# A second, grouped load of x and 32x32 block turns on VectorE for the covariance sums of a two-layer kernel

## The chip, the cores and the metric

The kernel runs on one core of a Trainium2 chip. The metric is the device time of one execution in microseconds. The core has TensorE (PE in the profile, with its weight loads as PEld), VectorE (DVE), ScalarE (ACT), GpSimd (POOL) and SyncE (SP), which here issues nearly all DMAs.

## The reference, cut to what matters

x is (8, 256, 96, 96) in float32: 8 images of 256 channels and 96 x 96 points. Two layers are computed, each added to its input.

```python
# layer 0, on n = groupnorm(x), 32 groups of 8 channels
q, k, v = (fft2(conv1x1(n, w, b)) for (w, b) in ((w1, b1), (w2, b2), (w3, b3)))
q, k = unit_length(q), unit_length(k)            # over the 9216 points of a channel
attn = einsum('bhcn,bhdn->bhcd', q, k) * temperature      # 8 heads of 32 channels
attn = complex(softmax(real(attn)), softmax(imag(attn)))
out = abs(ifft2(einsum('bhcd,bhdn->bhcn', attn, v)))
x = x + conv1x1(out, w_out)
# layer 1, on n = groupnorm(x): linear attention over points
q, k = softplus(conv1x1(n, Wq, bq)), softplus(conv1x1(n, Wk, bk))     # 32 channels
v = conv1x1(n, Wv, bv)
x = x + (q @ (k @ v)) / (q . sum(k))
```

The kernel never makes a Fourier transform of the points. For layer 0 it needs two things from x: the covariance of the channels, of x with itself and of x with x mirrored in both axes (point (h, w) against (-h, -w)), from which the softmax is worked out; and an image y, each row of x multiplied by a 96 x 96 table of that row.

## The kernel before, in words

**Stages.** Each image b goes through five stages. `pair_sums(b)` makes the covariance from even and odd sums of x and its mirror. `attention(b)` turns it into the small matrix mz, woven with `rotate(b)`, which makes y. `images(b)` multiplies y by mz (z, L747), squares, adds and takes roots (e, L788, L792, L793, L794), projects by wo (po, L759) and adds to x (L761). `layer1(b)` makes keys and queries (kq, L844), their softplus, transposed x (xT, L907), and kx (L885). `output(b)` multiplies out (o, L997), adds to x (L1002 on VectorE; L1005 and L1006 on ScalarE and GpSimd) and stores (L1016). `weave` advances one generator by the numbers that the other yields: `pair_sums(b + 1)` runs between the steps of images, layer1 and output of image b, and `rotate(b)` between the steps of `attention(b)`. x and y of an image lie in two arenas that change roles with each image.

**Sums.** x lies in SBUF with channels on partitions and its rows permuted (`x_col`), so that a block of 8 rows holds four rows and their mirrors. In each of 37 steps an image, GpSimd or ScalarE copies the mirrored part (`back`, L381), TensorE transposes front and back (eoT, L403 and L404), ScalarE evicts both (L405, 128x512), VectorE (L419) and GpSimd (L417) make sum and difference, and eight records of products (acc, L337) add up. `bn_stats` on VectorE (L290) takes the statistics of layer 0's norm, and layer 1's. For b > 0 the evicted rows of part of the image (blocks t of 4 and above) are spilled to DRAM (xtd, L409), and the column w = 0 is collected, transposed and spilled apart. The last sums of an image come after its output stage, in a tail of five steps.

**Rotation.** The order of rows is the hand-written list `pieces`. A row that was spilled comes back from DRAM (xT<-xtd, L648); any other one is transposed by TensorE (xr, L662) and evicted by ScalarE (L675). A y matmul (L665) uses the row and its table tm, which in image 0 comes as a window of rt or rb in DRAM and is written to rx, and later is read from rx (L620). Evictions take y (L671) and an extra column (ys, L670).

**Order.** The DMAs of SyncE are issued in the order of the code on one queue. DVE and POOL have a written order in image 0's sums, PE and POOL in attention and rotation, and all five engines in output and the tail; in images and layer1 a scheduler sets it. At the start come the loads of x (L143), the tables with the small loads and wo (`tables`, `load_small`, L233).

**Layer norm.** `group_norm` waits for bn_aggr (mv, L299), and its matmuls gm and gv (L306, L308) average over groups. layer1 begins with it (gm_b), attention too (gm_a).

Of the kernel before, what the change touches and what calls it, by code (L numbers as in the profile page):

```python
# [57 lines left out]
P = 128  # L58
# [5 lines left out]
T0 = 4  # L64
# [8 lines left out]
def two_layer_kernel(ctx: ExitStack, tc: tile.TileContext, x, w1t, b1, w2t, b2, w3, b3, wot, temp,  # L73
# [11 lines left out]
    assert C == KC * P and H == W and TW == 2 * CH and NT == 2 * NS and NC == 2 * NT and W <= P and H % TR == 0  # L85
# [12 lines left out]
    arenas = [const.tile([P, KC, HW], F32, name=f"arena{i}") for i in range(2)]  # L98
# [7 lines left out]
    def x_col(h):  # L106

        if h < H // 2:
            t, r = divmod(h, PR)
        elif h == H // 2:  # L110
            t, r = 0, 2 * PR - 1
        else:
            t = (H - h) // PR
            r = 2 * PR - 1 - (H - h) % PR
        return ((NT - 1 - t) * ROWS + r) * W

    def chunk_rows(c):

        t, half = NT - 1 - c // 2, c % 2
        if not half:  # L120
            return [(PR * t, PR)]
        return [(H - PR * t - PR + 1, PR)] if t else [(H - PR + 1, PR - 1), (H // 2, 1)]

# [3 lines left out]
    def ring_tile(name):  # L127
        return ring.tile([P, 6 * C], F32, tag="ring", name=name)
# [4 lines left out]
    loaded = set()  # L133

    def load_x(b, t):
        loaded.add((b, t))
        if (b, t) == (0, NT - 1):
            for h in (H // 2 - PR, H // 2 + PR - 1, H // 2 - 2, H // 2 + 1):
                nc.sync.dma_start(out=x_of(b)[:, :, x_col(h):x_col(h) + 2 * W], in_=x_v[b, :, :, h * W:(h + 2) * W])
            return  # L140
        for c in (2 * (NT - 1 - t), 2 * (NT - 1 - t) + 1):
            for h, n in chunk_rows(c):
                nc.sync.dma_start(out=x_of(b)[:, :, x_col(h):x_col(h) + n * W], in_=x_v[b, :, :, h * W:(h + n) * W])  # L143
# [4 lines left out]
    for t in range(NT - 1, -1, -1):  # L148
        load_x(0, t)
# [23 lines left out]
    turn = [0]  # L173

    def sum_slot():

        turn[0] += 1
        return xT[:, NX - 2 + turn[0] % 2]


# [7 lines left out]
    pw = const.tile([P, 4], F32, name="pw")  # L188
    nc.vector.memset(pw[:, 3:4], 0.0)
    for j in range(4):  # L190
        nc.vector.memset(pw[32 * j:32 * j + (16, 16, 17, 1)[j], 3:4], 1.0)
        if j != 2:
            nc.vector.memset(pw[32 * j:32 * j + 1, 3:4], 0.5 ** 0.5)
    nc.vector.scalar_tensor_tensor(pw[:, 3:4], in0=ident[:, 80:81], scalar=0.5 ** 0.5 - 1.0, in1=pw[:, 3:4],
                                   op0=ALU.mult, op1=ALU.add)
    for j in range(3):
        nc.vector.tensor_scalar(pw[:, j:j + 1], ident[:, 95 - 32 * j:96 - 32 * j], scalar1=-1.0, scalar2=1.0,
                                op0=ALU.mult, op1=ALU.add)
    nc.vector.tensor_sub(pw[:, 2:3], pw[:, 2:3], ident[:, P - 1:P])
# [47 lines left out]
    rb = dram.tile([H, 2 * W], F32, name="rb")  # L247
    rx = dram.tile([H // TR, W, TR, W + 1], F32, name="rx")

    xtd = dram.tile([2, (H // 2 - PR * T0 + 1) * W, C], F32, name="xtd")  # L250

    def tables():
# [18 lines left out]
        for i in range(2):  # L271
            o = (3 + i) * W
            nc.vector.tensor_copy(t0[:, o:o + 1], r0[:, 0:1])
            nc.vector.tensor_copy(t0[:, o + 1:o + W], r0[:, W - 1:0:-1])
            nc.sync.dma_start(out=rb[:, i * W:(i + 1) * W], in_=r0)
        nc.sync.dma_start(out=rt, in_=t0[:, 3 * W:5 * W])
        load_small()

    def window(h, n, back):

        v = (rb if back else rt)[h:h + n, 0 if back else 1:]
        return bass.AP(v.tensor, v.offset, [[1, W], [2 * W, n], [1, W]])

    def turned(c, h, w):

        return xtd[c, (h - PR * T0) * W + w:]

# [4 lines left out]
    def new_stats(name):  # L292
        return two.tile([P, KC, NC, 6], F32, tag="st", name=name)
# [29 lines left out]
    def image(t):  # L323
        return t.rearrange("p k (h w) -> p k h w", w=W)

    s0 = {}
    evicted = {}

    def pair_sums(b):

        st0 = new_stats(f"st0_{b}")
        acc = [acc_tile(f"acc{c}_{b}") for c in range(2)]

        def products(t, np_, first, last):
            for c in range(2):
                for m in range(KC):
                    mm = nc.tensor.matmul(acc[c][:, m * C:m * C + (KC - m) * P], lhsT=t[0:np_, c, m * P:(m + 1) * P],  # L337
                                          rhs=t[0:np_, c, m * P:C], start=(first and m == 0), stop=(last and c == 1),
                                          skip_group_check=True)
                    if first and m:  # L340
                        tc.keep_in_program_order(mm)

        x = x_of(b)

        w0 = one.tile([P, KC, H + 1], F32, tag="ys", name=f"w0_{b}")
        nc.gpsimd.memset(w0[:, :, H // 2:H // 2 + 1 + PR * T0], 0.0)

        def sides(t, j):

            o = (NT - 1 - t) * TW + (t == 0) * W + 1 + P * j  # L350
            e = (NT - t) * TW - (t == 0) * W - 1 - P * j
            if t or j < 2:
                return [(0, P, x[:, :, o:o + P], x[:, :, e:e - P:-1])]
            m = H // 2
            rows = [x[:, :, x_col(h):x_col(h) + W] for h in (0, H // 2)] + [w0]
            if j == 2:
                return [(0, 32, x[:, :, o:o + 32], x[:, :, e:e - 32:-1])] + [
                    (32 * i + 32, 32, v[:, :, 1:33], v[:, :, W - 1:W - 33:-1] if i < 2 else w0[:, :, m + 2:m + 34])
                    for i, v in enumerate(rows)]

            return [(32 * i, 32, v[:, :, m:m + 32], v[:, :, m:m - 32:-1]) for i, v in enumerate(rows[0:2])] + [
                (64, 32, w0[:, :, 32:64], None), (64, 16, None, w0[:, :, m + 33:m + 49]), (80, 16, None, w0[:, :, m:m + 16]),
                (96, 32, rows[0][:, :, 0:32], rows[0][:, :, 0:32])]

        back = three.tile([P, TR * (W + 1)], F32, tag="tm", name=f"back_{b}")[:, 0:2 * C].rearrange(
            "p (i k n) -> p i k n", i=2, k=KC)

        def turn_back(i):

            t, j = steps[i]  # L370
            assert (b, t) in loaded
            if j == 0:
                xts.append(ring_tile(f"xt_{b}_{t}_{j}").rearrange("p (j c n) -> p j c n", j=3, c=2))
            ab = sides(t, j)
            ready = len(ab) == 1

            front = ab[0][2] if ready else xts[-1][:, j % 3, 0].rearrange("p (k n) -> p k n", k=KC)
            for p0, n, *v in ab:
                for c in range(ready, 2):
                    if v[c] is not None:  # L380
                        (nc.scalar.copy if b and t < 5 and (ready or not c) else nc.gpsimd.tensor_copy)(  # L381
                            (front, back[:, i % 2])[c][:, :, p0:p0 + n], v[c])
            if j == 0:
                col = x[:, :, (NT - 1 - t) * TW:(NT - t) * TW:W]
                h, o = PR * t, H // 2 + 1 + PR * t
                nc.gpsimd.tensor_copy(w0[:, :, h:h + PR], col[:, :, 0:PR])
                if t:
                    nc.gpsimd.tensor_copy(w0[:, :, o:o + PR], col[:, :, :PR - 1:-1])
                else:
                    nc.gpsimd.tensor_copy(w0[:, :, o:o + 1], col[:, :, 0:1])  # L390
                    nc.gpsimd.tensor_copy(w0[:, :, o + 1:o + PR], col[:, :, 2 * PR - 2:PR - 1:-1])
                    nc.gpsimd.tensor_copy(w0[:, :, o - 1:o], col[:, :, 2 * PR - 1:])
            return front, xts[-1][:, j % 3]

        steps = [(t, j) for t in range(NT - 1, -1, -1) for j in range(3)] + [(0, 3)]
        pending, first = None, True
        xts = []
        ahead = turn_back(0)
        for i, (t, j) in enumerate(steps):
            front, both = ahead  # L400
            pt = ps_tile(f"eoT_{b}_{t}_{j}").rearrange("p (c n) -> p c n", c=2)
            for k in range(KC):
                nc.tensor.transpose(pt[:, 0, k * P:(k + 1) * P], front[:, k], ident)  # L403
                nc.tensor.transpose(pt[:, 1, k * P:(k + 1) * P], back[:, i % 2, k], ident)  # L404
            nc.scalar.activation(both, pt, AF.Copy, scale=pw[:, j:j + 1])  # L405
            evicted[0] = both
            if b and t >= T0:
                for c in range(2):
# [198 lines left out]
    def rotate(b):  # L607
# [88 lines left out]
        for p in pending:  # L696
            step(None, p)
# [404 lines left out]
```

## Time and profile before

| | us |
|---|---|
| median of 3 runs | 2705.23 (2702.59 to 2705.66) |
| profiled execution, span | 2700.8 |
| what lies around the span (median less span) | 4.4 |
| PE busy in it | 2659.0 (98%) |
| DVE, ACT, POOL busy | 1916.3, 1357.6, 889.3 |
| image 0: sums start, end; rotation ends | 10.3, 78.8, 152 |
| image 1: attention and rotation | 421.9 to 484.9 |
| image 1: images; layer 1; output; tail of the sums | to 624; 630 to 702; 711.5 to 744.3; to 753.6 |
| attention starts of images 2 to 7 | 753.6, 1084.2, 1414.9, 1745.6, 2076.9, 2407.8 |
| DMA, mean over the span | 105 GB/s, 33.8% of 16 engines |

From one attention to the next it is 330.7 us. The span is the time from the first to the last instruction of one execution. An engine is busy while one of its instructions runs; matmuls overlap, so that the busy time of a single matmul is longer than the step it takes. Lines such as L337 are those of the kernel before. A line of a group has the instruction's output and inputs by the program's names, its shape and count, then busy time and mean ns, then the idle time of the engine ahead of it, with what released it.

### The profile page before, as it was taken

Reading aid. Unit: us, or ns where it says so; the run is one execution under the profiler, and the core shown is the slowest. Engines: PE = TensorE matmul, PEld = TensorE weight load, DVE = VectorE, ACT = ScalarE, POOL = GpSimd, SP = SyncE. Lnnn points to the kernel's source line nnn. Section 1 sums busy time; section 2 is a strip of 40 time slices with the busy share of each in tenths; the row PEclk is TensorE's granted clock in tenths of the full one; section 3 lists DMA queues with packets and bytes.
Section 4 is the critical chain, followed back from the end, with each engine's and each line's share of the span. In section 5 each row is a group of like instructions: output and inputs, shape, how many; then the busy total and the mean of one; then the engine's idle time right before and its main releaser. Section 6 shows DMA issues by size and latency. Waiting matters only on the chain. (4 is left out here: it accounts for less than half of the span.)

```text
span 2700.8 us, 47703 instructions
## 1 busy us (share of the span) xinstructions
PE 2659.0 (98%) x17494; PEld 1905.6 (71%) x17494; DVE 1916.3 (71%) x4092; ACT 1357.6 (50%) x2167; POOL 889.3 (33%) x1335
## 2 busy tenths in 40 slices
PE   8999999999999999999999999999999999999988
PEld 8965678656796567956778567785677856778546
DVE  5678576785768757687666876769657687576766
ACT  3455553456535565355642556435464355644554
POOL 6133431334313344044340442404424134241311
PEclk9999999999999999999999999999999999999997
DMA  5220166302662026520364203641037411373003
GB/s 177 67 60 18 62 191 208 87 12 69 215 182 67 11 81 232 152 71 17 97 221 135 70 26 102 225 134 54 30 105 236 122 48 38 105 240 86 1 7 141
DMA packets 243183, 283.59 MB, mean 105 GB/s; under 512 B 37380, under 2 KB 231240, under 8 KB 242952
## 3 DMA queue, kind: packets, MB, share of 16 engines
q1 hardware_dynamic: 242008, 280.22, 33.8%
q8 instruction: 140, 2.29, 0.4%
q14 instruction: 91, 0.75, 0.1%
q10 hardware_dynamic: 944, 0.34, 0.0%
HBM read 156.76 MB, written 123.72 MB: 104 GB/s over the span
## 5 line engine op out<-in xcount | busy, mean ns | idle before, releaser
L747 PE MATMUL z<-arena,mz 128*128 128x384 f32 (+2 forms) x2400 | 595.0, 476 | 0.0
L793 POOL TENSOR_TENSOR e<-e 128x768 f32<-128x768 f32 x192 | 348.4, 1815 | 553.7 <-ACT e L792 550.1
L759 PE MATMUL po<-e,wo 128*128 128x384 f32 x1536 | 529.8, 486 | 0.2 <-ACT e L794 0.2
L747 PEld LDWEIGHTS z<-arena,mz 128*128 128x128 f32 (+1 forms) x2400 | 325.6, 163 | 241.4 <-issue 42.4
L337 PE MATMUL acc<-xT 128*128 128x256 f32 (+1 forms) x2368 | 448.3, 330 | 2.8 <-POOL xT L417 1.8
L759 PEld LDWEIGHTS po<-e,wo 128*128 128x128 f32 x1536 | 289.4, 190 | 197.7 <-DVE arena L761 1.2
L788 DVE TENSOR_TENSOR e<-z,xT 128x768 f32<-128x768 f32 x384 | 365.8, 953 | 85.4 <-PE z L747 85.3
L290 DVE BATCH_NORM_STATS2 st<-arena 128x6 f32<-128x384 f32 x768 | 410.4, 553 | 12.6 <-DMA arena<-in_x_dram 2.0
L337 PEld LDWEIGHTS acc<-xT 128*128 128x128 f32 x2368 | 382.7, 191 | 45.2 <-DVE xT L419 6.2
L665 PE MATMUL y<-tm,xT 96*128 96x97 f32 x3040 | 406.4, 270 | 3.6 <-DMA xT<-xtd 1.6
L665 PEld LDWEIGHTS y<-tm,xT 96*128 96x128 f32 x3040 | 395.5, 192 | 20.5 <-issue 12.1
L794 ACT ACTIVATE e<-e 128x768 f32<-128x768 f32 x192 | 162.0, 844 | 336.1 <-POOL e L793 333.9
L792 ACT ACTIVATE e<-e 128x1536 f32<-128x1536 f32 x192 | 284.5, 1482 | 91.8 <-DVE e L788 90.3
L405 ACT ACTIVATE xt<-eoT,pw 128x512 f32<-128x512 f32 x296 | 203.5, 688 | 182.9 <-PE eoT L404 171.1
L417 POOL TENSOR_TENSOR xT<-xt 128x256 f32<-128x256 f32 x352 | 256.5, 745 | 72.7 <-ACT xt L405 71.1
L761 DVE TENSOR_TENSOR arena<-arena,po 128x384 f32<-128x384 f32 x384 | 211.1, 552 | 90.9 <-PE po L759 67.7
L670 DVE COPY ys<-y 128x4 f32<-128x4 f32 (+1 forms) x384 | 61.4, 161 | 160.6 <-PE y L665 159.0
L1006 POOL TENSOR_TENSOR arena<-arena,po 128x384 f32<-128x384 f32 x96 | 96.3, 1003 | 232.4 <-ACT po L1005 229.6
L381 POOL COPY back<-arena 128x256 f32<-128x256 f32 (+1 forms) x230 | 84.7, 374 | 267.2 <-PE eoT L404 255.3
L671 DVE COPY arena<-y 128x384 f32<-128x384 f32 (+1 forms) x314 | 171.4, 546 | 1.4 <-issue 1.4
L419 DVE SCALAR_TENSOR_TENSOR xT<-eoT,pw,xt 128x256 f32<-128x256 f32 x240 | 107.2, 478 | 87.9 <-ACT xt L405 87.8
L1002 DVE TENSOR_TENSOR arena<-arena,o 128x384 f32<-128x384 f32 x288 | 142.4, 549 | 38.3 <-PE o L997 38.2
(235 smaller groups left out, 3316.0 us busy)
## 6 DMA issues: line engine op xcount, KB each, us to landing
out_dram<-arena SPq DMA_DIRECT2D x184, 384.0 KB
arena<-in_x_dram SPq DMA_DIRECT2D x182, 384.0 KB
xtd<-xt SPq DMA_DIRECT2D x336, 128.0 KB
xT<-xtd SPq DMA_DIRECT2D x217, 192.0 KB
tm<-rx SPq DMA_DIRECT2D x106, 218.2 KB
rx<-tm SPq DMA_DIRECT2D x16, 218.2 KB
tm<-rt SPq DMA_DIRECT2D x16, 216.0 KB
arena<-in_x_dram SPq DMA_DIRECT2D x8, 288.0 KB
```

What stands on the lines that cost most here:

```text
L290: nc.vector.bn_stats(out=st[:, k, c, :], in_=x_of(b)[:, k, c * CH:(c + 1) * CH])
L337: mm = nc.tensor.matmul(acc[c][:, m * C:m * C + (KC - m) * P], lhsT=t[0:np_, c, m * P:(m + 1) * P], rhs=t[0:np_, c, m * P:C], start=(first ...
L405: nc.scalar.activation(both, pt, AF.Copy, scale=pw[:, j:j + 1])
L417: on_pool(eo[:, c], both[:, 0], both[:, 1])
L665: nc.tensor.matmul(pu[:, o:o + W + 1], lhsT=gt[0:W, 1 - r if back else r, k * P:(k + 1) * P], rhs=tm[:, g % TR + r, :], start=True, stop=True)
L671: (nc.scalar.copy if on_scalar else nc.vector.tensor_copy)(y[:, :, :, g + r:g + 2], src[:, :, 0:W, r:2] if back else src[:, :, W - 1::-1, ...
L747: mm = nc.tensor.matmul(out[:, o:o + n * W], lhsT=columns(mz, k, c, j), rhs=y[:, k, h * W:(h + n) * W], start=(k == 0 and o == 0), stop=(k ...
L759: nc.tensor.matmul(po[:, 0:CH], lhsT=wo[:, k, m * P:(m + 1) * P], rhs=e[:, k, :], start=(k == 0), stop=(k == KC - 1))
L761: nc.vector.tensor_add(x[:, m, n], x[:, m, n], po[:, 0:CH])
L788: nc.vector.tensor_add(e[:, 2 * c:2 * c + 2, :].rearrange("p t (q h) -> p t q h", h=H), pz[:, 0:CH].rearrange("p (q h) -> p q h", h=H).uns ...
L792: nc.scalar.activation(e, e, AF.Square)
L793: nc.gpsimd.tensor_add(e[:, 0:2, :], e[:, 0:2, :], e[:, 2:4, :])
```

## The change: what it does

x is read from DRAM a second time, for the sums alone, in another layout. A "grouped" load puts 32 channels of one block on 32 partitions, and four rows, 12 apart, on the four groups of 32 partitions (`load_grouped`): for each of six v one gets two rows of each group forward (runs of 768 bytes) and their mirrors (runs of 384 bytes), 12 DMAs, and GpSimd copies the wrap column. VectorE turns 32x32 blocks (`turn_blocks`), two instructions of 128x768 for each u, after which rows of points lie on partitions. Both results are written to DRAM (xtd), and a pair of GpSimd and VectorE instructions make sum and difference, 128x768. There are 12 u of three products steps each, and a last step for the middle row: 37 steps, as before.

Gone are eoT and its evictions, the back copies, the spilling of part of the rows, the x permutation, rb, the windows, bn_stats for layer 0, xr and its evictions. The norm of layer 0 comes from acc, which gets a column of ones for the channels' sums, and the diagonal of the covariance. In the rotation every row comes from xtd and the tables from rx; all tables are written in image 0's `tables`. x itself is loaded in natural order during the rotation (8 blocks) and images (4). y has one more column, which takes the place of ys.

```diff
+    def load_grouped(b, v):
+        f, g = staged(b, v)
+        xs = x[b].rearrange("(c i) h w -> i c h w", i=32)
+        if 2 * v == NG:
...
+            nc.gpsimd.tensor_copy(g[0:32, :, 31:32], f[0:32, :, 0:1])
+            return
+        for a in range(G):
+            h, s = NG * a + 2 * v, slice(32 * a, 32 * a + 32)
+            nc.sync.dma_start(out=f[s].rearrange("p c r w -> p c (r w)"), in_=xs[:, :, h:h + 2].rearrange("p c r w -> p c (r w)"))
+            for r in range(2):
+                nc.sync.dma_start(out=g[s, :, r, 0:W], in_=xs[:, :, (H - h - r) % H])
+        nc.gpsimd.tensor_copy(g[:, :, :, W], g[:, :, :, 0])
...
     def tables():
...
-            nc.sync.dma_start(out=rb[:, i * W:(i + 1) * W], in_=r0)
         nc.sync.dma_start(out=rt, in_=t0[:, 3 * W:5 * W])
+        for i in range(NP + 1):
+            n = TR if i < NP else 1
+            tm = tm_tile(f"tm0_{i}")
+            v = rt[TR * i:TR * i + n, 1:]
+            nc.sync.dma_start(out=tm[:, 0:n, 1:W + 1], in_=bass.AP(v.tensor, v.offset, [[1, W], [2 * W, n], [1, W]]))
+            nc.gpsimd.tensor_copy(tm[:, 0:n, 0:1], csn[0:W, 2, TR * i:TR * i + n].unsqueeze(2))
+            nc.gpsimd.tensor_scalar_mul(tm[:, 0:n, W + 1:W + 2], tm[:, 0:n, 0:1], -1.0)
+            if i < NP:
+                for q in range(NQ):
+                    nc.sync.dma_start(out=rx[i].rearrange("(j q) r w -> q j r w", q=NQ)[q], in_=tm[32 * q:32 * q + 32])
...
         load_small()
...
+        def turn_blocks(u):
+            v, r = divmod(u, 2)
+            f, g = staged(b, v)
+            ft, gt = turned_pair(b, u)
+            if u < NG:
+                for t, src in ((ft, f[:, :, r, :]), (gt, g[:, :, r, W:0:-1])):
+                    nc.vector.transpose(out=t.rearrange("p (q c i) -> p q c i", q=NQ, c=NB8),
+                                        in_=src.rearrange("p c (q w) -> p q c w", q=NQ))
+                for c, t in enumerate((ft, gt)):
+                    nc.sync.dma_start(out=xtd[c, u], in_=t)
...
+            if r and v + 2 <= NG // 2:
+                load_grouped(b, v + 2)
+        def pair(u):
...
+            nc.gpsimd.memset(eo[0:np_, 0:nq, :, 0:CB:CB - 1], 1.0 if u < NG else R2)
...
+                nc.gpsimd.tensor_add(e, ft, gt)
+                (nc.gpsimd if b and u % 2 else nc.vector).tensor_sub(o, ft, gt)
+            return eo, nq, np_
+        turn_blocks(0)
+        ahead = pair(0)
+        turn_blocks(1)
+        for u in range(NG + 1):
+            eo, nq, np_ = ahead
+            for q in range(nq):
+                if q == 0 and u < NG:
+                    ahead = pair(u + 1)
+                if q == 1 and u + 2 <= NG:
+                    turn_blocks(u + 2)
...
+                products(eo, q, np_, u == 0 and q == 0, u == NG)
+                yield
...
     def rotate(b):
...
+        tms[0] = load_r(0)
+        tms[1] = load_r(1)
+        for i in range(3):
+            fetch(i)
+        yield
+        for i in range(len(order)):
+            step(i)
             fetch(i + 3)
+            if i % 6 == 3 and i // 6 < NT - 4:
+                load_x(b, i // 6)
             yield
...
     def images(b):
...
+            if i % 2 == 0 and i // 2 < 4:
+                load_x(b, NT - 4 + i // 2)
+            if b + 1 < B and i in (14, 17):
+                load_grouped(b + 1, (i - 14) // 3)
...
             weave(output(b, *l1.pop(b)), sums)
+            finish(sums)
             if b + 1 < B:
                 turns = rotate(b + 1)
-                finish(sums)
+                next(turns)
```

## The prediction

> **What bounds the kernel now.** I read the page's busy line first, then the slices, the costliest groups, the waits, windows by stage, and the timeline of TensorE.
>
> ```profile
> PE 2659.0 (98%) x17494; PEld 1905.6 (71%) x17494; DVE 1916.3 (71%) x4092; ACT 1357.6 (50%) x2167; POOL 889.3 (33%) x1335
> ...
> DMA  5220166302662026520364203641037411373003
> ```
>
> TensorE is busy 98% of 2700.8 us, and its largest wait in the table of waits is 6.2 us in all. So it alone sets the end; work taken from it is time gained, and any idle it gets is time lost. DMA is quiet in most slices but reaches 5 to 7 tenths where images change.
>
> The removed TensorE work, by tile:
>
> ```profile
> L662 PE MATMUL xr<-ident,arena 128*96 128x128 f32 x652 | 167.4, 275 | 0.0
> L403 PE MATMUL eoT<-ident,arena 128*128 128x128 f32 x560 | 147.7, 291 | 5.2 <-DMA arena<-in_x_dram 5.0
> L404 PE MATMUL eoT<-ident,back 128*128 128x128 f32 x592 | 146.6, 274 | 1.6 <-POOL back L381 1.6
> ```
>
> Matmuls are pipelined, so 275 ns is no step; distances between starts count, from the timeline:
>
> ```profile
> 18.74 0.27 PE L403 MATMUL eoT<-ident,arena 128*128 128x128 f32 x1
> ...
> 19.18 1.47 PE L337 MATMUL acc<-xT 128*128 128x256 f32 x8
> 20.49 0.27 PE L403 MATMUL eoT<-ident,arena 128*128 128x128 f32 x1
> ```
>
> A step of the sums takes 1.75 us: four transposes 0.44 (18.74 to 19.18) and the products 1.31.
>
> Windows of image 1 and of the change to image 2 (columns: length, then busy us of PE, PEld, DVE, ACT, POOL, clock, DMA share, GB/s):
>
> ```profile
> 422.00:484.00 62.00, 60.52 (x507) 56.63 (x505) 37.69 (x134) 19.14 (x40) 2.09 (x12) 1.00 0.61 168
> ...
> 706.00:744.00 38.00, 37.86 (x262) 26.50 (x260) 31.57 (x69) 17.37 (x37) 22.34 (x39) 1.00 0.81 277
> 744.00:754.00 10.00, 9.83 (x66) 8.55 (x63) 6.83 (x14) 5.00 (x15) 6.79 (x20) 1.00 0.87 291
> ```
>
> In turn: attention with the rotation; the output stage; its tail of sums. The DMA engines are 81 to 87% busy in the last two; dividing rate by share, the queue would saturate at 275 GB/s with the rotation's mix (168/0.61), 342 with the output's, 334 with the tail's. The reader should see that the change adds transfers where the queue is fullest.
>
> [...] L788, 128x768, takes 953 ns. [...]
>
> **The change, part by part.**
>
> *Gain on TensorE.* Sums: 37 steps x 0.44 = 16.1 us an image. Rotation: image 0 transposes all rows (190 records, 79 to 152, 73 us), image 1 has 66 in 62 us: 11/124 = 0.09 us each. So images 1 to 7 gain 66 x 0.09 = 5.9, image 0 17. That is 22.0 x 7 = 154, and 33 in image 0. The products' extra column (257 wide for 256) is under 0.4%: nothing.
>
> *VectorE, ScalarE, GpSimd in all.* The sums' norm leaves VectorE (half of L290's 410 us), as do L419's 107 and L670's 61. Added are some 200 turns (8 x 25) at 0.95 = 190 us (bounds 0.55, the 384-element copy L671 at 546 ns, and 1.8, if the strided read costs double), some 50 differences of 0.95 to 1.8, and more evictions. VectorE stays near its 71%, ScalarE loses L405's 203 us. On totals nothing new bounds; what matters is what stands ahead of what.
>
> *Image 0.* A pass is two groups u, six steps, 6 x 1.31 = 7.9 us of TensorE. But staged buffers alternate, so the loads for v+2 are issued only after the odd group's turn, and in GpSimd's written order the copy of the wrap column (line 158 of the changed kernel), which waits for these loads, stands before the next pair's sum, and before the memset that VectorE's difference waits for. The loop is: last turn 1.9; 12 issues at 0.39 (the 32 loads of wo took 12.34 us) 4.7; landing 2.1 (the fetch issued at 756.14 was used at 758.2); copy 0.4; sum 1.8 (L793: 1815 ns for 128x768); memset and difference 1.0; turn 1.9: 13.8 us. Over five passes 5 x 5.9 = 29. The tables' nine pieces stand in the same queue: a window, its copy on GpSimd, three writes, about 3.6 us each, 32 us, then wo's 12.3; sums can run some 12 us ahead: 32 more. From a first product at about 14: 14 + 37 x 1.31 + 29 + 32 = 124 where now 78.8: +45. With the rotation's -17: **+28** (bounds 0 and +60).
>
> *Head of layer 1, seven images.* VectorE's order now has pair 0, turns 2 to 4 and differences ahead of the bn_aggr whose result the gm_b matmul (L306) waits for: 6 x 0.95 + 3 x 0.95 = 8.6 us; GpSimd did both sums there. About 1.4 of chain after it, less three steps of products, 3.9: **+6** (1 to 10). [...]
>
> *Output stage.* GpSimd's copy for the middle row (line 151 of the changed kernel) waits for six fresh loads, 6 x 0.39 + 2.1 = 4.4 us plus queueing behind 1.57 MB of output rows; each fourth addition (L1006) and the odd pairs stand behind it: **+3** (1 to 6).
>
> *Start of the rotation.* Behind the last output rows (1.57 MB) in SP's queue come wl (0.79 MB), two tables (0.45) and the first rows (0.4), 3.2 MB: 11 us at 291 GB/s. The tail's cover shrinks from 9.3 us (744.3 to 753.6) to 5 x 1.31 = 6.6. Before, the first rows were turned by TensorE from SBUF, so nothing was needed. 11 - 6.6 = 4.4, landing 2.1, some 1 for a cold clock: **+7.5** (3 to 12).
>
> *Through the rotation.* All 49 steps now fetch: 49 x 192 KB, eight load_x of 768, nine tables of 223: 17.6 MB in binary, 18.0 decimal. At 291 GB/s 62 us, at 275 65, at 342 53. TensorE's need is 62 - 5.9 = 56. Slots prefetch only three to six steps: **+6.5** (0 to 10).
>
> *Covered.* The sums' norm from acc: some eight small VectorE instructions ahead of gm_a, about 2.7 us; woven y steps cover it, else +2.7 an image. The wrap copies of the first two groups, in the images stage, stand between additions L793 whose engine idles 553.7 us before them: nothing, else 2 to 4 us each. load_x into the arena in the rotation has no reader until images: nothing but its bytes, counted above.
>
> Sum for an image: -22.0 + 6 + 3 + 7.5 + 6.5 = +1.0, times 7 = +7, and +28: 2700.8 + 35 = 2736. The median of the runs lies 4.4 above the span: 2740.
>
> **The rivals.**
>
> *The stalls are covered (faster).* One mechanism decides: the queue keeps up. If it moves the rotation's 18.0 MB at 342 GB/s or more, that part takes 53 us under TensorE's 56, the fetches are early, and the start costs 4; with 3 at the head and 2 in the output about 9 an image remain: (9 - 22) x 7 = -91, image 0 +20: 2705.2 - 71 = 2634. It turns at 28/7 = 4 us an image below the gain: with stalls under 18 us an image the kernel is faster. For: output and tail imply over 330; the table shows few waits of y for xT (1.6 us). Against: the rotation's mix implies 275, and those 1.6 us had 22 fetched steps, not 49.
>
> *The queue saturates (much slower).* At 275 or less, [...] rotation +10, start +12, output +6, head +8: 36 an image, (36 - 22) x 7 = +98, image 0 +40: 2843. For: 81 to 87% before anything is added. Against: the grouped loads are spread over some 100 us.
>
> **How the numbers follow.** Forecast (small net loss, 2712 to 2795) 0.46; saturated (2795 to 2870) 0.21; covered (2590 to 2699) 0.28; between, within 0.2% of before, about what a measurement of this kernel can tell from no change, 0.05. Faster 0.28, same 0.05, slower 0.67. The range leaves a tenth out at each end: 2620 to 2840. The cases of slower alone: 2712 to 2840.
>
> **What would show it.** Right: no eoT and xr records; sums at 1.31 us a step; sums of image 0 ending near 124; PE waits at gm_b for mv_b, and at the first y for xT from xtd, of 5 us or more an image; DMA share in the rotation near 1; PE's busy share near 91% (2659 - 187 of 2736). Wrong: image 0's sums ending before 100, a period from sums to sums well under 320 us (now 330.7), or turns far from 0.95 us: at 1.8 VectorE would hold up the head and the sums too.

## The result, and the profile after

| | us | ratio to before, 95% interval |
|---|---|---|
| before | 2705.3 | |
| after | 2973.6 | 1.098 [1.094, 1.101] |

The change makes the kernel 268 us slower. Slower was forecast, but at 2740 and at most 2840. The profiled execution has a span of 2977.4 us. These are its lines of engines, granted clock and DMA on the page:

```profile
PE 2713.5 (91%) x15580; PEld 1931.7 (65%) x15580; DVE 1793.2 (60%) x3294; ACT 1118.8 (38%) x1658; POOL 777.5 (26%) x783
...
PEclk8779997799977999779996899979998799977998
DMA  8673247633386344852457424774157723476003
```

TensorE has 1914 fewer matmul records and is busy for 54.5 us more. Busy time that grows while the work shrinks means slower instructions, and the row PEclk, the share of its full clock that TensorE was granted, says why: before it stood at 9 in all slices but the last (a mean of 0.994), now it dips to 6 or 7 in each image (a mean of 0.896). A stretch at half clock is called cold below. The same shows in the groups (busy us, mean ns, idle before), here with the new transposes:

```profile
L614 PE MATMUL y<-tm,xT 96*128 96x97 f32 x3072 | 523.3, 345 | 116.2 <-DMA xT<-xtd 116.2
...
L339 PE MATMUL acc<-eo 128*128 128x257 f32 (+2 forms) x2368 | 467.1, 346 | 81.4 <-POOL eo L373 68.6
...
L353 DVE STREAM_TRANSPOSE arena<-arena 128x768 f32<-128x768 f32 x192 | 180.7, 959 | 32.9 <-POOL eo L383 22.9
```

The y matmul, unchanged in shape, takes 345 ns in place of 270. From the starts of the stages in both traces (images 2 to 6, mean us):

| | before | after | change | forecast |
|---|---|---|---|---|
| attention and rotation, to the first z | 62.8 | 86.6 | +23.8 | +0.6 |
| images to the end of layer 1 | 225.2 | 222.4 | -2.8 | -3.2 |
| output and tail of the sums | 42.8 | 50.2 | +7.4 | +3.5 |
| period | 330.8 | 359.2 | +28.4 | +1.0 |

(The forecast's 0.44 us a step are shared out by the steps of the sums in each stage before: 21 in the second row, 16 in the third.)

In image 0 attention, which follows the sums, starts at 148.4 us (79.5 before, +69 where +45 was forecast; this start stands for the end of the sums below), and the rotation takes 75.4 us (71.9 before; 17 less was forecast). So most of the loss lies in the rotations. The windows of image 1: rotation, images, output, tail and start of the next rotation (columns as in the prediction's windows; the DMA share can come out above 1):

```profile
499.00:586.00 87.00, 79.38 (x443) 73.82 (x442) 26.79 (x71) 20.40 (x37) 0.20 (x2) 0.70 0.74 219
590.00:731.00 141.00, 139.88 (x530) 81.47 (x528) 113.08 (x172) 72.22 (x79) 56.24 (x40) 0.99 0.26 61
...
811.00:843.00 32.00, 31.65 (x191) 20.95 (x190) 25.35 (x47) 5.26 (x11) 20.79 (x24) 1.00 0.79 279
843.00:861.00 18.00, 7.91 (x47) 7.14 (x43) 5.23 (x15) 0.96 (x2) 1.88 (x6) 0.73 1.03 316
```

In the rotation TensorE idles 7.6 of 87 us and DMA is 74% busy: neither is full. What is low is the clock, 0.70. The timeline of TensorE there:

```profile
496.99 2.85 PE L614 MATMUL y<-tm,xT 96*128 96x97 f32 x12 [10.30 <-DMA xT<-xtd]
...
502.52 7.12 PE L614 MATMUL y<-tm,xT 96*128 96x97 f32 x32
...
516.77 1.96 PE L469 MATMUL cw<-wl,scr 128*128 128x512 f32 x2
...
520.19 1.95 PE L469 MATMUL cw<-wl,scr 128*128 128x512 f32 x4
521.97 1.03 PE L614 MATMUL y<-tm,xT 96*128 96x97 f32 x8
```

After a wait of 10.3 us, 32 y records take 7.12 us (0.22 each, back to back: nothing is waited for). After the wide cw matmuls of attention, 8 take 1.03 (0.11 to the next instruction). The trace's clock records have the granted clock at one half from 489.5 for 30.7 us (it falls within the wait of 10.3), from 544.2 for 20.5 (at the end of a wait of 3.5) and from 574.9 for 17.1 (within the second of two waits, of 1.9 and 2.3). In the first stretch y records, with a few small matmuls of attention between them, run for 20 us and don't end it; it ends 3.5 us after the first cw, the second with mz (264 wide), the third with zs and z.

My first theory was then that of the **clock**: waits for rows, each short, halve TensorE's clock, and the narrow y stream can't win it back. The rival is the **queue**: late rows pace the rotation, and the clock only follows.

### The profile page after: what moved, and what is told of

It is laid out like the page before. It is cut to its first block, busy times and chain, and to the rows that moved or that the text cites. A ratio compares the mean times of both kernels' runs of the same rounds, so it can differ in the third digit from the quotient of the medians.

```text
span 2977.4 us, 41809 instructions
## 1 busy us (share of the span) xinstructions
PE 2713.5 (91%) x15580; PEld 1931.7 (65%) x15580; DVE 1793.2 (60%) x3294; ACT 1118.8 (38%) x1658; POOL 777.5 (26%) x783
## 4 chain that ended last, share of the span: by engine, by line
PE 78%; DMA 8%; DVE 6%; SPq 2%; issue 2%; POOL 2%; ACT 1%; POOLq 0%; ACTq 0%; DVEq 0%
PE z L676 19%; PE po L684 15%; PE y L614 14%; PE acc L339 10%; DMA xT<-xtd 5%; PE kq L771 4%; PE o L916 4%; PE xT L832 3%; PE kx L810 2%; DMA arena<-in_x_dram 1%; DVE arena L803 1%; POOL eo L382 1%; PE cw L469 1%; DVE arena L353 1%; POOL eo L383 1%
## 5 line engine op out<-in xcount | busy, mean ns | idle before, releaser
L614 PE MATMUL y<-tm,xT 96*128 96x97 f32 x3072 | 523.3, 345 | 116.2 <-DMA xT<-xtd 116.2
L676 PE MATMUL z<-arena,mz 128*128 128x384 f32 (+1 forms) x2304 | 602.5, 506 | 0.0
L339 PE MATMUL acc<-eo 128*128 128x257 f32 (+2 forms) x2368 | 467.1, 346 | 81.4 <-POOL eo L373 68.6
L339 PEld LDWEIGHTS acc<-eo 128*128 128x128 f32 (+1 forms) x2368 | 389.8, 198 | 207.4 <-issue 89.0
L619 ACT COPY arena<-y 128x388 f32<-128x388 f32 (+1 forms) x192 | 122.3, 637 | 547.2 <-PE y L614 469.9
L295 DVE BATCH_NORM_STATS2 st<-arena 128x6 f32<-128x384 f32 x384 | 210.6, 554 | 10.3
L353 DVE STREAM_TRANSPOSE arena<-arena 128x768 f32<-128x768 f32 x192 | 180.7, 959 | 32.9 <-POOL eo L383 22.9
L382 POOL TENSOR_TENSOR eo<-arena 128x768 f32<-128x768 f32 x88 | 174.8, 1986 | 7.0 <-DVE arena L353 1.0
L832 PE MATMUL xT<-ident,arena 128*128 128x128 f32 x1152 | 148.7, 278 | 6.0 <-DVE xT L837 3.4
L832 PEld LDWEIGHTS xT<-ident,arena 128*128 128x128 f32 x1152 | 128.7, 143 | 23.2 <-issue 10.7
```

Of the source, the lines that this page charges most:

```text
L295: nc.vector.bn_stats(out=st[:, k, c, :], in_=x_of(b)[:, k, c * CH:(c + 1) * CH])
L339: mm = nc.tensor.matmul(acc[c][:, m * (C + 1):m * (C + 1) + C + 1 - m * P], lhsT=eo[0:np_, q, c, 1 + m * P:1 + (m + 1) * P], rhs=eo[0:np_, ...
L353: nc.vector.transpose(out=t.rearrange("p (q c i) -> p q c i", q=NQ, c=NB8), in_=src.rearrange("p c (q w) -> p q c w", q=NQ))
L614: nc.tensor.matmul(pu[:, o:o + W + 1], lhsT=xt[:, s, k * P:(k + 1) * P], rhs=tm[:, h % TR + s, c:c + W + 1], start=True, stop=True)
L619: (nc.scalar.copy if i % 2 else nc.vector.tensor_copy)(y[:, :, :, g:g + nr], src if c else src[:, :, W::-1, :])
L676: nc.tensor.matmul(out[:, 0:CH], lhsT=columns(mz, k, c, j), rhs=y[:, k, i * CH:(i + 1) * CH], start=(k == 0), stop=(k == KC - 1), skip_gro ...
```

## The experiments

All times are medians on the chip. Each kernel is the changed one with the edit shown, but for the one on the kernel before.

**Fillers ahead of the rotation.**

```diff
+                fill = ps_tile(f"fill_{b}")
+                for _ in range(22):
+                    nc.tensor.matmul(fill, lhsT=ident, rhs=wo.rearrange("p k o -> p (k o)"), start=True, stop=True)
                 turns = rotate(b + 1)
```

> Edit: between the tail of the sums and the first y step of images 1 to 7, where TensorE idles some 10 us, 22 matmuls of 128x512 are added whose result nobody reads (22 x 0.44 us = 9.7 us). Rows arrive no earlier. Clock theory (the idle halves TensorE's clock and the narrow y matmuls, 97 columns wide, don't win it back for 20 us and more): the cold stretch of 30.7 us at the start of each rotation goes; about 22 us of work in it ran at half speed, so about 10 us an image, 70 in all: 2890 to 2920 us, granted clock in the first 20 us of the rotation 1.0. Queue theory (the rotation is paced by rows that come late, and the clock only follows): 2960 to 2980, no shorter rotation than the 82 us of the changed kernel.

Measured 2910.8 us, 1.075 [1.072, 1.077]: 63 less, with 154 matmuls more. The rotation falls from 82 to 67 us; the tail grows by 7, since one such matmul takes 0.88 us and not 0.44 (a matmul shows as two records, of which I had counted one; in the run with five fillers below, five show as 10 records over 4.46 us). The first cold stretch is gone in the clock records. The fillers also hold the first y back by 8 us, in which rows can come; but if rows set the pace, a later start could at best leave the end where it was, and it comes 9 us an image earlier. Clock theory, within its numbers.

**Wide fillers in the rotation, and narrow ones.**

```diff
             pu = ps_tile(f"y_{b}_{c}_{h}")
+            if i % 2 == 0:
+                nc.tensor.matmul(pu, lhsT=ident, rhs=wo.rearrange("p k o -> p (k o)"), start=True, stop=True)
```

> Edit: each second y step gets one 128x512 matmul ahead of its own four, overwritten by them: 25 x 0.44 = 11 us more of TensorE work in each rotation. Clock theory: [...] of some 53 cold us in a rotation 30 to 35 go, saving 16 and costing 11: 2900 to 2960 us, although more work is done; granted clock in the rotation over 0.85 (now 0.70). Queue theory: the work is hidden in waits at best and added at worst: 2980 to 3060, clock below 0.8.

```diff
             pu = ps_tile(f"y_{b}_{c}_{h}")
+            for _ in range(4 if i % 2 == 0 else 0):
+                nc.tensor.matmul(pu[:, 0:W + 1], lhsT=xt[:, 0, 0:P], rhs=tm[:, h % TR, c:c + W + 1], start=True, stop=True)
```

> Edit: as with the wide fillers, but each second y step gets four more matmuls of its own narrow kind (97 columns) in place of one of 512: about the same 0.44 us of TensorE at full clock. Clock theory, that width counts: the clock isn't won back, each filler costs 0.44 to 0.88 us, 25 x 8 of them: 3060 to 3150 us, clock in the rotation 0.7 or below. Theory that any TensorE work wins the clock back: as the wide fillers, 2900 to 2960. Queue theory: 2980 to 3060.

The wide ones: 2941.5 us, 1.087 [1.086, 1.089], 32 us *less* although each rotation has 22 us more work. The narrow ones: 3023.5 us, 1.118 [1.116, 1.119], 50 us more. Their windows in image 1's rotation, wide and then narrow:

```profile
501.00:583.00 82.00, 82.00 (x487) 65.78 (x487) 27.01 (x71) 20.45 (x37) 0.20 (x2) 0.90 0.73 222
```

```profile
510.00:601.00 91.00, 91.00 (x636) 85.51 (x635) 26.75 (x72) 20.60 (x37) 0.21 (x2) 0.82 0.63 194
```

TensorE is busy throughout in both. In image 1's clock records the first cold stretch lasts 23.9 us with wide fillers and 41.0 with narrow ones (30.7 with none). Where it ends says more than its length. With wide fillers it is over before attention's first cw in all seven rotations of images 1 to 7. With narrow ones cw comes later than without fillers (in image 1, 24 us after attention's start in place of 17), and the stretch lasts until 3 to 8 us behind it in all seven. So narrow work doesn't win the clock back, as the clock theory says; whether by its 97 columns or by its 96 rows (128 in the wide matmuls) wasn't separated. It is the clock records that decide here: the time of the narrow ones lies in the queue theory's range and below the clock theory's. Both kinds also remove the later stretches, probably since slower steps let rows come in time, and my numbers for the narrow ones were too high for that reason.

**x loaded behind the rotation.**

```diff
-            if i % 6 == 3 and i // 6 < NT - 4:
-                load_x(b, i // 6)
...
-            if i % 2 == 0 and i // 2 < 4:
-                load_x(b, NT - 4 + i // 2)
+            for t in ((0, 1, 2) if i == 0 else (i // 2 + 2,) if i % 2 == 0 and i // 2 + 2 < NT else ()):
+                load_x(b, t)
```

> Edit: the loads of x in natural order leave the rotation; all but two or three of the twelve blocks are issued behind the last row of the rotation. 4.7 of the rotation's 18 MB go. Queue theory: rows come in time after the start, the rotation falls from 82 to about 65 us: 2840 to 2870. Clock theory: the start is as before (30 us cold), the two later cold stretches shrink or go as their stalls go: 70 to 74 us, 2890 to 2930. If the bytes in the rotation didn't matter: 2970 to 2980.

Measured 2808.0 us, 1.038 [1.036, 1.039]: 166 less, more than either theory had. The rotation takes 64 us, the start is as cold as before (30.7 us in six of the seven images), and no other cold stretch is left in it. So the eight 768 KB loads between the fetches made the later waits (7.6 us in image 1), and these cost far more in clock than they lasted. Both theories have a part: the queue makes the wait, the clock multiplies it. Whether the size of a single load or their bytes in all made the waits was not separated.

**The start on another queue.** wl, two tables and the first six rows, three of them asked for earlier, from ScalarE's queue (nc.scalar.dma_start for b > 0):

> Edit: for images 1 to 7 the three weight loads, two tables and the first six rows of the rotation are issued by ScalarE's DMA queue instead of behind the last output rows in SyncE's. [...] Queue-order theory (the start waits because it stands behind 1.6 MB of output rows in one queue): TensorE's idle at the start falls from 10.3 to 5 us or less; alone -5 x 7 = 2935 to 2950[...]. Bandwidth theory (the bytes need their 10 us whoever issues them): 2965 to 2985.

Measured 2939.5 us, 1.087 [1.084, 1.090]. Output and tail fall from 50 to 45 us, but the rotation stays at 79 to 85 us, with a first cold stretch of 27 to 31: the idle is shorter (5 to 6 us in place of 10 to 12), and the clock drops all the same. Queue order held a part of the start, and not its clock.

**Image 0.** GpSimd's wrap copy just ahead of its turn, and (apart) the tables and small loads on ScalarE:

```diff
-        nc.gpsimd.tensor_copy(g[:, :, :, W], g[:, :, :, 0])
...
             ft, gt = turned_pair(b, u)
+            if r == 0 and u < NG:
+                nc.gpsimd.tensor_copy(g[:, :, :, W], g[:, :, :, 0])
```

> Edit: GpSimd's copy of the wrap column is written just ahead of the turn that reads it, in place of right behind the loads, so that it no longer stands ahead of the next pairs' sums. All images. Theory of the GpSimd order (image 0: passes of 18 us against 8 of products): three to four passes lose 6 to 8 us each: image 0's sums end 20 to 30 us earlier, 2940 to 2955 us. If loads are the limit (12 issues and their landing after the odd turn): under 5 us, 2965 to 2975. Other images within 2 us.

> Edit: the tables' chain (rt, nine windows, 25 writes, two small copies each) and the small loads with wo are issued and done by ScalarE, idle in image 0's sums, in place of SyncE and GpSimd. Theory of the queue (from 64 to 106 us SyncE issues nothing for the sums, and TensorE waits 26.7 and 22.0 us): image 0's sums end 35 to 50 us earlier: 2920 to 2940. If the passes' own loop bounds: 10 to 20 us, 2955 to 2965.

Measured 2940.9 us, 1.087 [1.085, 1.090], and 2931.5 us, 1.083 [1.081, 1.085]. Image 0's sums end at 135 and at 142 us (148 in the changed kernel): 13 and 7 earlier, less than I had for either. That both totals lie in the ranges of the theories which had promised more of the sums is luck. The rest of the first one's gain is 3 us in each later image, where I had expected no change; the rest of the second one's lies in the rotations, image 0's above all (75 to 66 us).

**All four together.**

> Edit: four edits together: x loaded behind the rotation, the start of the rotation on ScalarE's queue, wrap copies late, tables and small loads on ScalarE. Clock and queue theories together: from 2808 (x behind the rotation) image 0 takes 60 to 80 off, the start 5 x 7 = 35, and 10 x 7 more if the start no longer cools the clock: 2640 to 2715, about the kernel before or better. If the edits only shift one wait to another: 2740 or more.

Measured 2780.8 us, 1.027 [1.025, 1.029]: the effects don't add. Image 0's sums end at 124.5, but each rotation of a later image still starts with 27 us of cold clock, though the idle is down to 3.1 us and 1.6 us shortly after (image 2).

**With five fillers, and four more in the first steps.** The four edits together once more, but with the wrap copies late in image 0 alone and the small loads back on SyncE:

> Edit: x behind the rotation, the rotation's start on ScalarE's queue, wrap copies late in image 0 alone, the tables' chain on ScalarE (small loads and wo stay on SyncE), and five wide matmuls without a reader between the sums' tail and the first y step of images 1 to 7 (five take about 4 us, what is left of the idle there). If the clock is the greatest loss: from 2781 with the same edits without fillers, 27 cold us at each start go, 10 x 7 = 70, and 2 x 7 in the output: 2690 to 2715. If fillers only move the wait: 2770 to 2790.

> Edit: as the last combined version (x behind the rotation, start on ScalarE's queue, wrap copies, tables on ScalarE, five fillers before the rotation), and one 128x512 matmul without a reader ahead of each of the first four y steps of images 1 to 7 (4 x 0.88 us at full clock). In that version the clock still drops for 20.5 us a few us into each rotation, after waits of 0.9, 1.1 and 1.1 us among narrow matmuls. Clock theory: with wide work among these waits the clock holds; 10 us saved, 3.5 spent, less what hides in the waits: 6 to 9 us an image, 2710 to 2730. If rows set the pace: 2770 to 2795.

Measured 2769.9 us, 1.023 [1.022, 1.025], and 2780.3 us, 1.030 [1.026, 1.034]. The clock theory's numbers failed in both; the second time lies where rows setting the pace had been expected. The clock still drops for 20.5 us a few us into the rotation. With the start on ScalarE's queue, ScalarE stands at these DMAs (8.4 us for six rows in the trace of all four together) and reaches its part of the norm late: with four more fillers the gv_a matmul waits 2.6 us for ScalarE's dv_a. They cost their time and the clock drops all the same, for 17 to 21 us.

**The same idle in the kernel before.**

```diff
                 finish(sums)
+                stall = ring_tile(f"stall_{b}")[:, 0:3 * C]
+                nc.gpsimd.memset(stall, 0.0)
+                for _ in range(6):
+                    nc.gpsimd.tensor_add(stall, stall, stall)
+                ps = ps_tile(f"stalled_{b}")
+                nc.tensor.matmul(ps[:, 0:P], lhsT=ident, rhs=stall[:, 0:P], start=True, stop=True)
```

> Edit, on the kernel before: ahead of the first rotation step of images 1 to 7, one 128x128 matmul that needs the last of six dependent GpSimd additions of 128x768, whose result nobody reads: TensorE idles some 6 to 8 us there, as in the changed kernel, all else being as before. If one idle of that length costs what it lasts [...]: 7 to 9 us an image, 2755 to 2770. If the rotation can't win the clock back here either: 15 to 18 us an image, 2810 to 2835, with a cold stretch of 20 us and more at each rotation's start.

Measured 2804.4 us, 1.037 [1.035, 1.040]. The timeline shows the idle, and the window after it (image 2) the clock:

```profile
773.13 0.80 PE L1057 MATMUL stalled<-stall,ident 128*128 128x128 f32 x2 [8.72 <-POOL stall L1055]
```

```profile
775.00:838.00 63.00, 62.19 (x513) 58.35 (x512) 37.53 (x133) 19.42 (x40) 0.20 (x2) 0.98 0.52 144
```

An idle of 8.7 us costs 14 us an image: 10 ahead of attention, some 4 through the rotation. The cold stretch lasts 10.2 us in this image and 10 to 17 over the seven, and ends 4 to 11 us after work is taken up again, in each before the first cw. In the changed kernel it is 30.7 in each of the seven and ends 21 to 23 us after. One difference between the two streams is the xr transposes, 128 wide, which are woven into the first steps before and which the change removed. That they bring the clock back is argued from this comparison; no run put them into the changed kernel. Neither of my two numbers fits: the time lies between them, nearer the second.

**x behind the rotation, and fillers to cover the whole idle.** As with x loaded behind the rotation, eleven fillers (11 x 0.88 us) ahead of it, wrap copies late in image 0, tables on ScalarE; the start stays with SyncE.

> Edit: x behind the rotation, wrap copies late in image 0 alone, the tables' chain on ScalarE, and eleven wide matmuls without a reader (11 x 0.88 = 9.7 us) in the idle of 10.3 us ahead of the rotation of images 1 to 7; the start stays on SyncE's queue, so that ScalarE is free for the norm's chain. Clock theory: the bytes that stalled the rotation are gone and the clock enters it full, so no cold stretch is left in it: rotation 54 to 57 us, 8 to 10 us an image less than with x behind the rotation alone (2808), and 18 less in image 0: 2715 to 2735. If the clock drops all the same at the first small wait: 2770 to 2790.

Measured 2740.1 us, 1.014 [1.011, 1.017], the best of the changed design, just above the 2735 expected at most. In four of seven images no cold stretch is left; in three one of 17 to 21 us comes back. Windows of two rotations, and a line of the timeline:

```profile
458.00:515.00 57.00, 56.70 (x485) 52.95 (x489) 26.78 (x72) 20.29 (x37) 0.20 (x2) 1.00 0.85 233
785.00:842.00 57.00, 56.11 (x473) 52.48 (x476) 26.66 (x72) 20.13 (x37) 0.20 (x2) 1.00 0.86 236
```

```profile
808.10 11.83 PE L620 MATMUL y<-tm,xT 96*128 96x97 f32 x104
```

At full clock a y record takes 0.114 us, the rotation 54 to 56 us, and the period is 327 to 328 us in four images (330.8 before). What makes this kernel slower than the one before is image 0: its sums end at 132 us, 52 later, and the rest of the profiled execution is 20 us shorter.

**Why image 0 stays late.** On top of the last version, four staging buffers in place of two in image 0, with four groups loaded at the start; then also the small loads and wo behind the tables on ScalarE:

```diff
-        r = x_of(b)[:, v % 2, 0:LO]
+        r = x_of(b)[:, v % 2, 0:LO] if b or v % 4 < 2 else y_of(b)[:, v % 2, 1024:1024 + LO]
...
-            if r and v + 2 <= NG // 2:
-                load_grouped(b, v + 2)
+            D = 2 if b else 4
+            if r and v + D <= NG // 2:
+                load_grouped(b, v + D)
```

> Edit: the last version (x behind the rotation, wrap copies late in image 0, tables on ScalarE, eleven fillers), and in image 0 four staging buffers in place of two (the two more in the other arena, free there), so that loads run four groups ahead. Theory that the two buffers set image 0's pass (load only after the turn): sums end 20 to 35 us earlier, at 97 to 112 (132 in the last version): 2705 to 2722. Theory that issues and bytes set it (72 loads at 0.45 us, 9.4 MB): under 10 us: 2730 to 2742.

> Edit: as with four staging buffers, and the small loads with wo are issued by ScalarE behind its tables, written three steps into the sums. If the small loads' 47 issues in SyncE's queue (some 19 us) stand ahead of writes that the turns wait for: 10 to 18 us less than with four buffers alone, 2688 to 2710, faster than the kernel before or the same. If the queue has room for them: within 4 us of it.

Measured 2758.5 us, 1.019 [1.017, 1.021], and 2776.2 us, 1.025 [1.022, 1.028]; the sums end at 136 us in both. Two buffers are not the limit. Windows of the first:

```profile
0.00:20.00 20.00, 4.37 (x15) 3.77 (x16) 8.96 (x31) 1.98 (x4) 4.25 (x67) 1.00 0.97 174
20.00:40.00 20.00, 6.46 (x39) 5.77 (x37) 0.67 (x2) 0.00 (x0) 2.06 (x3) 0.76 1.20 211
40.00:60.00 20.00, 14.10 (x73) 12.54 (x74) 13.68 (x33) 0.00 (x0) 10.39 (x11) 0.81 1.00 234
60.00:80.00 20.00, 4.18 (x24) 3.47 (x23) 1.97 (x7) 1.53 (x9) 0.00 (x0) 0.70 0.65 182
80.00:100.00 20.00, 9.86 (x48) 8.66 (x48) 5.00 (x6) 1.22 (x7) 5.41 (x5) 0.76 0.46 126
100.00:120.00 20.00, 5.01 (x17) 4.38 (x18) 8.47 (x10) 0.00 (x0) 6.37 (x6) 0.52 0.55 204
```

The DMA engines are full for 60 us, at 174 to 234 GB/s, and 46 to 65% busy in the next 60. The sums load 9.4 MB in groups and write 9.4 MB to xtd; at these rates 81 to 108 us, an estimate, whatever the order. But bytes don't explain the waits after 60 us. With eleven fillers and two buffers they are plain to see: a window of image 0, SyncE's issues and VectorE's next turn.

```profile
80.00:100.00 20.00, 0.00 (x0) 0.00 (x0) 0.00 (x0) 0.00 (x0) 0.26 (x2) 0.54 0.11 24
```

```profile
87.73 10.80 SPq L233 DMA_DIRECT2D wo<-in_wot_dram  x32
98.63 2.32 SPq L360 DMA_DIRECT2D xtd<-arena  x4
```

```profile
101.16 2.01 DVE L357 STREAM_TRANSPOSE arena<-arena 128x768 f32<-128x768 f32 x2 [32.58 <-DMA xtd<-arena]
```

For 20 us next to nothing runs and DMA is 11% busy: SyncE issues the small loads and wo, 53 DMAs from 77.5 to 98.5 us, and only then the writes to xtd that the turn waits for. With these loads moved to ScalarE, in the last run, SyncE's grouped loads wait 22.4 us for the tables' transfers of the other queue:

```profile
SPq L158 <- DMA tm<-rt: 22.4, 5, 4.8
```

So the order of the issues costs image 0 time that bytes don't explain: with all four edits together, where the small loads are ScalarE's, the sums end at 124.5 us, and with them back on SyncE at 130.8. What else holds image 0 is open. Why the last run is slower still, in its later rotations too (59 to 64 us), I did not settle.

## Why the prediction was wrong

**Right, in part by luck.** A turn takes 959 ns (0.95 forecast, from L788's 953). TensorE's gain is there where the clock is full: with x behind the rotation and eleven fillers it takes 54 to 56 us (forecast: 5.9 less than 60 to 62), image 0's 55.6 in place of 71.9 (-16, forecast -17). Images to the end of layer 1 came out at -2.8 (forecast -3.2), but the wait in it is half of the forecast 6: PE waits 22.9 us in eight images for mv_b at gm_b, 2.9 each, where 5 or more had been named as the sign:

```profile
PE gm_b L311 <- DVE mv_b L304: 22.9, 8, 2.9
```

The rest of what the row lost lies elsewhere: a step more of the sums before output (1.3), a wait at po (1.0), up to 6.8 us at half clock around gm_b. PE's share of 91%, another sign, came out as forecast by chance: 2713.5 us of 2977.4, not 2472 of 2736. The idle at the rotation's start was forecast as 6.5 us before the clock; it is 10.3. Two slips in the working change nothing: 37 x 0.44 is 16.3, not 16.1, and the fetch issued at 756.14 had landed at 758.2, but no y matmul used it then.

**The step that failed** is "some 1 for a cold clock", together with "through the rotation: +6.5". I took the clock for a small surcharge on a wait. From attention's start to the first z the change costs 23.8 us an image where +0.6 was forecast, most of the 28.4 in all. In image 1 the rotation takes 31 us more than at full clock (86 against 55): 7.6 are idle, the other 24 are mostly work at half speed, in stretches of 31, 21 and 17 us that waits of 10, 3.5 and 4 us began. The clock records of both kernels hold two speeds, 1.0 and 0.5. In the changed kernel the stretches at half last 3.4, 6.8, 13.7, 17.1, 20.5, 27.3 or 30.7 us, all multiples of 3.4, but for the last one, which the end of the execution cuts off. Of the way back they show this: y records, with attention's small matmuls between them, run from 497.0 to 516.8 us in image 1 at a granted clock of 0.50; the clock is back 1.8 to 3.5 us after the first cw (128x512) in each of images 1 to 7. What it is in the work that decides was not shown. I had read that TensorE was at full clock in nearly the whole profile of before (three stretches at half clock, of 3.4, 3.4 and 29.2 us, all behind 2609 us), and so saw no price for leaving it. Nor did I ask whether the removed transposes were part of what brings it back, as the idle put into the kernel before suggests.

**Image 0** (+28 forecast, +78 measured: 69 in the sums, where 45 were forecast; 3.5 in the rotation, where 17 were to be gained; the rest behind it). The chain of GpSimd is there; its waits, in the changed kernel's timeline, are these:

```profile
16.81 6.68 PE L339 MATMUL acc<-eo 128*128 128x257 f32 x24 [12.26 <-DVE eo L379]
36.45 11.04 PE L339 MATMUL acc<-eo 128*128 128x257 f32 x48 [12.96 <-POOL eo L373]
54.47 10.57 PE L339 MATMUL acc<-eo 128*128 128x257 f32 x48 [6.98 <-POOL eo L373]
91.72 10.72 PE L339 MATMUL acc<-eo 128*128 128x257 f32 x48 [26.68 <-POOL eo L373]
124.39 22.91 PE L339 MATMUL acc<-eo 128*128 128x257 f32 x128 [21.95 <-POOL eo L373]
```

A pass takes 18 us (33.5 to 51.5 on GpSimd) where I had 13.8, and two waits lie around the tables (68.9 to 121.4). The lines add up to the end of the products, 147.3 where I had 124: the first product comes 3 us later, the four waits after it last 68.6 us in place of 61, and the 37 steps take 61.9 in place of 48.5. So the waits were nearly right, and the largest miss is again the clock, which stands at half for some 20 us of the products. Late copies and other queues together give back 15 to 24 of the 69 us; the cause of what is left stays open. I had priced the grouped loads by their issues, never by the rate at which they move, which fills the DMA engines in the first 20 us (a share of 0.98 at 174 GB/s).

**The rivals.** "The queue saturates" named the place and the sign of what the rotation lost, but as transfer time, 10 us an image; DMA was 74% busy. "The stalls are covered" is the way that x behind the rotation and fillers go: a period 3 to 4 us under the one before in four images, where this rival had 13.

## What to carry to other kernels

What a wait on TensorE cost depended here on the stream behind it: an idle of 8.7 us put into the kernel before cost 14 us an image, with 10 to 17 us at half clock; in the changed kernel one of 10 to 12 us began 30.7 us at half clock in each of seven images. Look at the row of the granted clock, and at what runs after each new wait: y records of 97 columns ran for 20 us at half clock, and after the first cw, of 512 columns, the full clock was back within 1.8 to 3.5 us. Work that is taken from TensorE may also be work that brings its clock back (argued here for the xr transposes, not shown); before removing it, ask what is left behind a wait. Eight loads of 768 KB put between fetches of 192 KB on one queue made waits of 1.9 to 3.5 us here (image 1), and without them the kernel was 166 us faster; put such transfers where no fetch is due. And in a queue that is issued in order, look for small DMAs that nobody needs yet ahead of writes that somebody waits for: 53 of them took SyncE 21 us here, and the turn behind them waited 32.6 us.

## What the runs showed of the hardware

- Wide matmuls without a reader in an idle of TensorE made the kernel 63 us faster (2973.6 to 2910.8), and put between the useful ones of the rotation 32 us faster (2941.5).
- Narrow y matmuls can keep a full clock that they don't win back: with x behind the rotation and fillers, 104 of them ran for 11.83 us at full clock (1.00 in that window); in the changed kernel they ran for 20 us at half (0.50).
- Loads onto 32 partitions at a time, in runs of 768 and 384 bytes, filled the DMA engines (0.97 with four staging buffers, 0.98 in the changed kernel, in the first 20 us) at 174 GB/s; the output stage moved 279 GB/s at 0.79. Which of partitions and run length does it wasn't tried.
- GpSimd's 128x768 addition takes 2.58 to 2.60 us in the changed kernel where VectorE's difference of the same two tiles (0.96 us) starts together with it, which is so in image 0 and once in each later image; it takes 1.80 to 1.84 in later images beside turns. What of the difference lengthens it was not shown.
